# Attention block in f32: the softmax division pinned behind the fifth key block's running sum, and v's products laid in seven of the fourth head's eight key blocks

## The chip, the cores and the metric

The kernel runs on one core of a Trainium2 chip. The metric is the device time of one execution in microseconds (us); lower is better. Times are medians of several runs of one program, and the profile is of one further execution of it.

The engines' names are those of the profile: PE is the tensor engine (PEld its weight loads), DVE the vector engine, ACT the scalar engine, POOL the GpSimd engine, SP the sync engine. A "q" behind the name means the engine's sequencer, for instance one that issues a DMA.

## The reference

A group norm, an attention with four heads of 128 channels over 1024 positions, an output projection and a residual, for a batch of 16:

```python
# x: (16, 512, 32, 32) float32
xn = group_norm(x, 8 groups) * gamma + beta
q, k, v = split(einsum('oc,bchw->bohw', qkv_w, xn) + qkv_b)   # four heads of 128
attn = softmax(einsum('bhnd,bhmd->bhnm', q, k) * 128 ** -0.5, axis=-1)
out = einsum('bhnm,bhmd->bhnd', attn, v)
return x + einsum('oc,bchw->bohw', proj_w, out) + proj_b
```

The softmax's division can be done last: with p = exp(score), a head's output is (sum over m of p v) times 1 / (sum over m of p). That final multiplication is what this document calls the division.

## The kernel before

One loop runs over 16 batches x 4 heads x 8 key blocks of 128 keys. In each key block PE makes the scores of this block in two halves of 512 queries, ACT takes their exponentials, DVE adds them to a running sum `tot`, and PE multiplies the exponentials of the block before with v (`po`). Between these stand the products of the projections, cut into small units. They are made by Strassen's scheme in two levels: 4 groups of 7 units, each with sums of inputs on DVE, products into one of two kinds of PSUM bank (`x` and `y`), and evictions on ACT and DVE. Which units a head carries:

- first head (h = 0): q and k of this batch's second pair of heads
- second head (h = 1): the output projection of the batch before, and the norm of the next batch
- third head (h = 2): q and k of the next batch's first pair of heads
- fourth head (h = 3): v of the next batch

The parts that matter here, cut:

```python
    def scores(s, half):
        b, h, j = where(s)
        sc = ps_s.tile([P, HALF], F32, tag="s", name=f"s_{s}_{half}")
        nc.tensor.matmul(
            sc, ks[b, h][:, ts(j, P)], qs[b, h][:, ts(half, HALF)], start=True, stop=True
        )
        # ... (ps[s]: a tile for the exponentials of this block)
        nc.scalar.activation(ps[s][:, ts(half, HALF)], sc, AF.Exp, scale=SCALE)
        # ... (the sum follows the second half)
        if j == 1:
            tot[b, h] = lpool.tile([P, N], F32, tag="tot", name=f"tot_{b}_{h}")
            nc.vector.tensor_add(tot[b, h], ps[s - 1], ps[s])
        else:
            nc.vector.tensor_add(tot[b, h][:, i], tot[b, h][:, i], ps[s][:, i])

    def denominators(b, h):
        # DVE: two transposes, a reduction, small sums and a reciprocal of tot -> r, 32 x 32
        # ...
        inverse[b, h] = r

    def spread_inverse(b, h, step):
        if step == 0:      # to DRAM as one row
            row = rows_of[b, h] = dpool.tile([1, N], F32, tag="row", name=f"row_{b}_{h}")
            nc.scalar.dma_start(
                row.rearrange("o (c i) -> (o c) i", i=BLK), inverse.pop((b, h))
            )
            return
        rinv[b, h] = lpool.tile([P, N], F32, tag="rinv", name=f"rinv_{b}_{h}")
        nc.scalar.dma_start(rinv[b, h], rows_of.pop((b, h)).to_broadcast((P, N)))

    def divide(b, h):
        nc.vector.tensor_mul(os_[b, h], os_[b, h], rinv.pop((b, h)))

    def spread(plan, units, first, last):
        for i, u in enumerate(units):
            plan[first + i * (last - first) // len(units)].append(u)
```

One unit of a projection, and what follows a group of units:

```python
            def inner_sum(m):           # sums of inputs, tiles qk_t, pp_t; v loads kept ones
                # ...
                for i in range(n):
                    nc.vector.tensor_sub(have[m][:, i, :], inner(i, a), inner(i, c))

            def out_(which, a, c=None):  # eviction of a bank, tiles qk_r, pp_r, v_r
                # ...
                if c is None:
                    nc.scalar.copy(dst, view(a))
                else:
                    nc.vector.tensor_add(dst, view(a), view(c))

            return [
                unit(weights, lambda: inner_sum("t1"), lambda: inner_sum("t2"), p1),
                unit(lambda: inner_sum("t3"), p2), unit(lambda: inner_sum("t4"), p6),
                unit(lambda: load(g + 1, "t2"), p5), unit(lambda: load(g + 1, "t1"), p7),
                unit(lambda: load(g + 1, "t3"), p4),
                unit(lambda: load(g + 1, "t4"), p3, end),
            ]
```

`weights` loads the group's weights from DRAM into one of two buffers. When v's groups are combined, each finished block goes through a sum (`vt`), a transpose on DVE (`vu`), a write to DRAM and two loads back (`v_groups`, cut here).

What a head carries, and the main loop:

```python
    def plan_head(b, h):
        plan = [[] for _ in range(NB)]
        if h == 0:
            spread(plan, staggered(next_qk.pop()), 0, NB)
            if b > 0:
                plan[6].append(lambda: o_blocks(b - 1))
                plan[6].append(lambda: sums_of_b(ob[b - 1]))   # DVE sums of o, the tiles ot
        # ...
        elif h == 2:
            spread(plan, staggered(qk_groups(b + 1, 0)), 0, NB)
        else:
            spread(plan, staggered(next_v.pop()), 0, NB)
        return plan

    for s in range(steps + 1):
        # ... (units = plan[j] of this head)
        if 0 < s < steps and s % NB == 0:
            denominators(*where(s - 1)[:2])
        for half in range(NH2):
            if s < steps:
                scores(s, half)
                if j == 1 and s > NB:
                    spread_inverse(*where(s - NB)[:2], half)
                if half == 0 and j == 5 and s > NB:
                    divide(*where(s - NB)[:2])
            if s > 0:
                weighted_sum(s - 1, half)
            n = (len(units) + 1) // 2
            run(units[half * n : (half + 1) * n])
```

So the division of a head is written in key block j = 5 of the head that follows it. The order in which an engine gets its instructions is not the written one: it is set when the kernel is built, by the operands' dependencies and the build's own estimate of when each instruction can go. `tc.issue_after(instruction)` adds a demand to it: what is written inside comes later than that instruction on its engine.

Of the kernel before, what the change touches and what calls it, by code (L numbers as in the profile page):

```python
# [154 lines left out]
def fast_path(ctx, tc, x, sources, out, consts, flag, dims):  # L155
# [6 lines left out]
    nc = tc.nc  # L162
    B, C, N, NCC, NH2, NB, GC, SCALE = dims
# [79 lines left out]
    def stats_group(b):  # L243
        mu, sc = norm.group(mvs.pop(b))
        scaled[b] = sc, norm.shift(mu, sc)
# [22 lines left out]
    def sums_of_b(b, rows=(1, 2), chunks=range(KC)):  # L268

        def sub(o, i, j):  # L270
            for k in chunks:
                nc.vector.tensor_sub(b[o][k], b[i][k], b[j][k])

        if 1 in rows:
            sub("t1", "b12", "b11")
        if 2 in rows:
            sub("t2", "b22", "t1")
            sub("t3", "t2", "b11")
            sub("t4", "b21", "t2")
# [6 lines left out]
    def o_blocks(b):  # L286
        ob[b] = halves([os_[b, h] for h in range(HEADS)], "o")
# [34 lines left out]
    def stage_blocks(site):  # L322

        raw = raw_blocks(site)
        st = stage[site] = {}
        names = ("a11", "a12", "a21", "a22", "s1", "s2")
        if site in ("proj", "v"):
            for n in names[:4]:
                st[n] = ypool.tile([P, HALF], F32, tag="y", name=f"st_{n}")
            for i, n in enumerate(names[4:]):  # L330
                st[n] = tpool.tile([P, HALF], F32, tag=f"ot2{i}", name=f"st_{n}")
        else:
            for i in range(3):
                t = opool.tile([P, N], F32, tag="o", name=f"st_{site}_{i}")
                for h in range(2):
                    st[names[2 * i + h]] = t[:, ts(h, HALF)]
        for n in names[:4]:
            load_block(st[n].rearrange("p (s d) -> p s d", d=P), raw[n])
# [66 lines left out]
    def run(units):  # L405
        for u in units:
            u()
# [270 lines left out]
    def proj_groups(b):  # L678

        def finish(which, r, a, c):  # L680
            of, half = int(which[1]) - 1, int(which[2]) - 1
            o = 2 * of + r
            t = ypool.tile([P, HALF], F32, tag="y", name=f"y_{b}_{o}_{half}")
            dma = nc.gpsimd.dma_start(t, x[b, ts(o, P), ts(half, HALF)])

            tc.add_manual_dep(
                dma.ins, last_eviction[b].ins.name,
                mybir.DependencyInfo(
                    mybir.DependencyClass.Sync, mybir.DependencyReason.DATA
                ),  # L690
                reason="residual",
            )
            nc.vector.scalar_tensor_tensor(
                t, a, projb_sb[:, o : o + 1], t, ALU.add, ALU.add
            )
            nc.vector.tensor_add(t, t, c)  # L696
            nc.gpsimd.dma_start(out[b, ts(o, P), ts(half, HALF)], t)  # L697

        return two_levels(f"pp_{b}", "proj", b, lambda: ob[b], finish)


    ps, tot, po, rinv, last_eviction = {}, {}, {}, {}, {}
    inverse, rows_of = {}, {}
    steps = B * HEADS * NB

    def where(s):
        bh, j = divmod(s, NB)
        return (*divmod(bh, HEADS), j)
# [7 lines that stand above are left out]
        if half == 0:  # L716
            ps[s] = ppool.tile([P, N], F32, tag="p", name=f"p_{s}")
        nc.scalar.activation(ps[s][:, ts(half, HALF)], sc, AF.Exp, scale=SCALE)  # L718
        i = ts(half, HALF) if s == steps - 1 else ds(0, N)
        if j == 0 or (half == 0 and s < steps - 1):  # L720
            return
        if j == 1:
            tot[b, h] = lpool.tile([P, N], F32, tag="tot", name=f"tot_{b}_{h}")
            nc.vector.tensor_add(tot[b, h], ps[s - 1], ps[s])
        else:
            nc.vector.tensor_add(tot[b, h][:, i], tot[b, h][:, i], ps[s][:, i])  # L726

    def denominators(b, h):

# [85 lines left out]
# [7 lines that stand above are left out]
# [20 lines left out]
    def staggered(lists):  # L842


        starts = (0, 4, 8, 16)[: len(lists)] if len(lists) != 3 else (0, 4, 10)
        at = [(a + i, g, u) for g, (a, us) in enumerate(zip(starts, lists))
              for i, u in enumerate(us)]
        return [u for _, _, u in sorted(at, key=lambda t: t[:2])]
# [98 lines left out]
# [7 lines that stand above are left out]
                plan[6].append(lambda: sums_of_b(ob[b - 1]))  # L954
            else:
                plan[5].append(lambda: stage_blocks("v"))
        elif h == 1:
            if b > 0:
                spread(plan, staggered(proj_groups(b - 1)), 0, NB)
            if b + 1 == B:  # L960
                plan[0].append(lambda: last_loads("x"))
            else:
                plan[0].append(lambda: load_x(b + 1))
                spread(plan, [lambda c=c: stats_chunk(b + 1, c) for c in range(NCC)], 2, 4)
                plan[4].append(lambda: stats_group(b + 1))
                for r in range(2):
                    plan[5 + r] += [
                        lambda c=c, half=half: normalise(b + 1, c, half)
                        for c in range(KC * r, KC * r + KC) for half in range(NH2)
                    ]  # L970
                    plan[6 + r].append(lambda r=r: x_sums(b + 1, (r + 1,)))
            if b == 0:
                for g in range(len(OUTER)):
                    plan[g // 2].append(lambda g=g: kept_group("v", g))
                    plan[NB // 2 + g].append(lambda g=g: kept_group("proj", g))
                plan[2].append(lambda: stage_blocks("proj"))
                spread(plan, [lambda o=o: bias_of_v(o) for o in range(NCC)], 3, 5)
        elif b + 1 == B:
            if h == 2:
                plan[0].append(lambda: last_loads("w"))  # L980
                plan[2].append(last_bias)
            else:
                os_[b, h] = opool.tile([P, N], F32, tag="o", name=f"o_{b}_{h}")
                plan[3].append(lambda: o_blocks(b))
                plan[3].append(lambda: sums_of_b(ob[b], (1,)))
                plan[5].append(lambda: sums_of_b(ob[b], (2,), (0,)))
        elif h == 2:
            spread(plan, staggered(qk_groups(b + 1, 0)), 0, NB)
        else:
            spread(plan, staggered(next_v.pop()), 0, NB)  # L990
        return plan

    def warm(n, name):
# [26 lines left out]
    next_v, next_qk = [], [qk_groups(0, 1)]  # L1020
# [3 lines left out]
    plan = []  # L1024
    for s in range(steps + 1):
        units = []
        if s < steps:
            b, h, j = where(s)
            if j == 0:
                plan = plan_head(b, h)  # L1030
            units = plan[j]
            if j == NB - 1 and h > 1 and b + 1 < B:
                (next_v if h == 2 else next_qk).append(
                    v_groups(b + 1) if h == 2 else qk_groups(b + 1, 1)
                )
                if h == 2:
                    units.append(ahead[f"v_{b + 1}"])
# [4 lines that stand above are left out]
                scores(s, half)  # L1042
                if j == 1 and s > NB:
                    spread_inverse(*where(s - NB)[:2], half)
                if half == 0 and j == 5 and s > NB:
                    divide(*where(s - NB)[:2])
            if s > 0:
                weighted_sum(s - 1, half)
            n = (len(units) + 1) // 2
            run(units[half * n : (half + 1) * n])  # L1050
        if s > 0:
            del ps[s - 1]
# [134 lines left out]
```

## Time and profile before

| what | value |
|---|---|
| time, median of 3 runs | 3317.27 us (3309.16 to 3321.45) |
| span of the profiled execution | 3309.1 us |
| PE busy | 3198.2 us, 97% |
| DVE busy | 2659.2 us, 80% |
| ACT busy | 1446.6 us, 44% |
| POOL busy | 527.0 us, 16% |
| granted clock of PE | 0.998 |

A row of the costliest groups names the line, the engine, the operation, the tiles written and read and their shape, how often, the busy time in us with the mean of one in ns, and behind the second bar how long the engine sat idle just before these instructions and what ended most of that. A row of the waits names the engine and tile that waited, what it waited for, the total in us, how many times, and the longest. A row of a timeline has the start and the length in us, the instruction, and in brackets the idle time before it with what ended it. A row of the stretches has the window, its length, the busy time and number of instructions of PE, PEld, DVE, ACT and POOL, the clock, the share of the DMA engines and GB/s. A product's record is longer than the distance to the next product, [...] so busy PE is not the same as PE at its peak.

### The profile page before, as it was taken

The page shows a single profiled execution, that of the slowest core. Times are in us where ns is not written, and L with a number is a line of the kernel's source. Part 1 is how long each engine was busy: PE and PEld are TensorE (multiplying, and loading weights), DVE is VectorE, ACT ScalarE, POOL GpSimd, SP SyncE. Part 2 cuts the span into 40 slices and gives each one's busy share as a digit, 9 for nine tenths or more (in the row PEclk, how much of TensorE's full clock was granted, in tenths as well). Part 3 has the DMA queues.
Part 4 walks back from the last instruction along what each step waited for, and adds up shares of the span by engine and source line. Part 5 has one row for each costly group of instructions (what it writes and reads, how often), then busy time and mean ns, then how long its engine had stood idle before and what let it go on. Part 6 is the DMA issues. An engine that isn't in the chain of part 4 may idle for free. (4 is left out here: it accounts for less than half of the span.)

```text
span 3309.1 us, 33607 instructions
## 1 busy us (share of the span) xinstructions
PE 3198.2 (97%) x10474; PEld 2165.8 (65%) x10474; DVE 2659.2 (80%) x4609; ACT 1446.6 (44%) x2709; POOL 527.0 (16%) x938
## 2 busy tenths in 40 slices
PE   8999999999999999999999999999999999999999
PEld 6566666666666666666666666666666666666664
DVE  8878878788887888878888787887878878788784
ACT  2534435344353443534435354353534535344342
POOL 1011121111211112111121101212012121121100
PEclk9999999999999999999999999999999999999999
DMA  5555454545535455454554545545355463454631
GB/s 202 196 187 151 169 177 145 168 150 172 176 133 171 144 172 177 154 159 139 171 174 154 172 136 179 170 147 179 127 176 175 144 204 126 160 162 162 189 124 39
DMA packets 172664, 530.54 MB, mean 160 GB/s; under 512 B 28864, under 2 KB 51904, under 8 KB 172480
## 3 DMA queue, kind: packets, MB, share of 16 engines
q1 hardware_dynamic: 91120, 276.86, 25.5%
q0 software_dynamic: 67392, 216.07, 20.3%
q10 hardware_dynamic: 13968, 35.41, 3.5%
q8 instruction: 85, 1.39, 0.2%
q14 instruction: 99, 0.81, 0.1%
HBM read 389.56 MB, written 138.67 MB: 160 GB/s over the span
## 5 line engine op out<-in xcount | busy, mean ns | idle before, releaser
L806 PE MATMUL po<-p,v 128*128 128x512 f32 x2048 | 1053.8, 596 | 0.0
L713 PE MATMUL s<-qk,qk 128*128 128x512 f32 x2048 | 1049.1, 594 | 2.9 <-ACT p L718 2.9
L718 ACT ACTIVATE p<-s 128x512 f32<-128x512 f32 x1024 | 610.5, 597 | 992.6 <-PE s L713 982.5
L806 PEld LDWEIGHTS po<-p,v 128*128 128x128 f32 x2048 | 600.8, 303 | 315.3 <-issue 197.6
L726 DVE TENSOR_TENSOR tot<-tot,p 128x1024 f32<-128x1024 f32 x385 | 470.4, 1222 | 116.6 <-ACT p L718 114.5
L713 PEld LDWEIGHTS s<-qk,qk 128*128 128x128 f32 x2048 | 388.2, 190 | 91.4 <-issue 28.7
L510 PE MATMUL qk_x<-qk_t,w 128*128 128x256 f32 x1344 | 361.5, 386 | 3.4 <-ACT qk_u L421 2.1
L510 PEld LDWEIGHTS qk_x<-qk_t,w 128*128 128x128 f32 x1344 | 246.1, 190 | 175.9 <-issue 65.4
L421 ACT COPY qk_u<-qk_x 128x512 f32<-128x512 f32 (+1 forms) x256 | 136.3, 533 | 287.5 <-PE qk_x L510 245.5
L499 POOL DMA_DIRECT2D kept_t<-qk_t x256 | 138.8, 543 | 491.2 <-DVE qk_t L495 457.1
L660 POOL DMA_DIRECT2D vd<-vu x120 | 66.5, 554 | 827.0 <-DVE vu L652 766.7
L529 DVE TENSOR_TENSOR qk_r<-qk_y,qk_u 128x512 f32<-128x512 f32 (+1 forms) x256 | 158.7, 620 | 47.4 <-ACT qk_u L421 26.4
L510 PE MATMUL pp_x<-pp_t,w_proj 128*128 128x256 f32 x630 | 173.9, 389 | 3.0 <-ACT pp_u L421 3.0
L529 DVE TENSOR_TENSOR v_r<-v_y,v_u 128x512 f32<-128x512 f32 (+1 forms) x120 | 75.1, 626 | 124.0 <-ACT v_u L421 116.3
L510 PE MATMUL qk_y<-qk_t,w 128*128 128x256 f32 x448 | 128.9, 393 | 45.9 <-DVE qk_t L495 30.6
L697 POOL DMA_DIRECT2D out_y<-y x120 | 66.4, 554 | 653.5 <-DVE y L696 620.7
L510 PEld LDWEIGHTS v_x<-v_t,w_v 128*128 128x128 f32 x630 | 118.4, 190 | 79.1 <-issue 38.3
L510 PE MATMUL v_x<-v_t,w_v 128*128 128x256 f32 x630 | 166.6, 381 | 0.0
L510 PEld LDWEIGHTS pp_x<-pp_t,w_proj 128*128 128x128 f32 x630 | 113.8, 190 | 69.8 <-ACT pp_u L421 24.8
L665 POOL DMA_DIRECT2D v<-vd x240 | 140.3, 592 | 52.1 <-issue 47.3
L510 PEld LDWEIGHTS qk_y<-qk_t,w 128*128 128x128 f32 x448 | 80.8, 191 | 101.6 <-DVE qk_t L495 41.4
L816 DVE TENSOR_TENSOR o<-o,rinv 128x1024 f32<-128x1024 f32 x63 | 77.0, 1223 | 86.7 <-DMA rinv<-row 86.7
(204 smaller groups left out, 4537.6 us busy)
## 6 DMA issues: line engine op xcount, KB each, us to landing
w<-kept SPq DMA_DIRECT2D x90, 896.0 KB, 6.1
kept_t<-qk_t POOLq DMA_DIRECT2D x192, 256.0 KB, 2.8
v_t<-kept_t SPq DMA_DIRECT2D x180, 256.0 KB, 2.7
w_v<-kept_v SPq DMA_DIRECT2D x45, 896.0 KB, 4.9
w_proj<-kept_proj SPq DMA_DIRECT2D x45, 896.0 KB, 4.5
rinv<-row ACTq DMA_DIRECT2D x63, 512.0 KB, 4.5
x<-in_x POOLq DMA_DIRECT2D x60, 512.0 KB, 5.7
vd<-vu POOLq DMA_DIRECT2D x120, 256.0 KB, 2.6
```

Source lines behind the costliest of these rows:

```text
L421: nc.scalar.copy(t[n][:, :width], t["x"][:, :width])
L499: nc.gpsimd.dma_start(t, have[m][:, :n])
L510: nc.tensor.matmul(acc[:, ts(i, Q)], have["w"][:, i, SLOTS[an], :], inner(i, bn), start=(first and i == 0), stop=True, skip_group_check=True,)
L529: nc.vector.tensor_add(dst, view(a), view(c))
L660: nc.gpsimd.dma_start(rows[which][ts(h, P), :], u)
L665: nc.gpsimd.dma_start(vs[b, pair][ts(q, BLK), half].rearrange("m h (k i) j -> m (h k) (i j)", k=n), rows[which].rearrange("(k m) (q e) -> ...
L697: nc.gpsimd.dma_start(out[b, ts(o, P), ts(half, HALF)], t)
L713: nc.tensor.matmul(sc, ks[b, h][:, ts(j, P)], qs[b, h][:, ts(half, HALF)], start=True, stop=True)
L718: nc.scalar.activation(ps[s][:, ts(half, HALF)], sc, AF.Exp, scale=SCALE)
L726: nc.vector.tensor_add(tot[b, h][:, i], tot[b, h][:, i], ps[s][:, i])
L806: nc.tensor.matmul(po[b, h][:, i], v_block(b, h, j), ps[s][:, i], start=(j == 0), stop=(j == NB - 1),)
L816: nc.vector.tensor_mul(os_[b, h], os_[b, h], rinv.pop((b, h)))
```

## The change

Two things. The division is written in key block 4, behind the second half's scores, and pinned on DVE behind the running sum of that block, so that it can come no earlier in DVE's order. It is meant to keep DVE from standing still in front of a division whose inverse is still on its way. And the 28 units of v, which were spread over all eight key blocks of the fourth head, are spread over the first seven, so that v's last sums and transposes on DVE come earlier against the start of the next batch.

```diff
     ps, tot, po, rinv, last_eviction = {}, {}, {}, {}, {}
-    inverse, rows_of = {}, {}
+    inverse, rows_of, added = {}, {}, {}
 ...
-            nc.vector.tensor_add(tot[b, h][:, i], tot[b, h][:, i], ps[s][:, i])
+            added[b, h, j] = nc.vector.tensor_add(
+                tot[b, h][:, i], tot[b, h][:, i], ps[s][:, i]
+            )
 ...
         elif h == 2:
             spread(plan, staggered(qk_groups(b + 1, 0)), 0, NB)
         else:
-            spread(plan, staggered(next_v.pop()), 0, NB)
+
+            spread(plan, staggered(next_v.pop()), 0, NB - 1)
 ...
-                if half == 0 and j == 5 and s > NB:
-                    divide(*where(s - NB)[:2])
+                if half == 1 and j == 4 and s > NB:
+
+                    with tc.issue_after(added[b, h, 4].ins):
+                        divide(*where(s - NB)[:2])
```

## The prediction

> **What bounds the kernel now.** I read the page's busy times first, then what the tensor engine (PE) waited for, then the four heads of one batch as stretches of time, then the timelines of PE and the vector engine (DVE) inside them. The page:
>
> ```profile
> PE 3198.2 (97%) x10474; PEld 2165.8 (65%) x10474; DVE 2659.2 (80%) x4609; ACT 1446.6 (44%) x2709; POOL 527.0 (16%) x938
> ...
> L816 DVE TENSOR_TENSOR o<-o,rinv 128x1024 f32<-128x1024 f32 x63 | 77.0, 1223 | 86.7 <-DMA rinv<-row 86.7
> ```
>
> PE is the bound and nothing in the change alters its products, so all that can be won is PE's idle time. Line 816 is the division: DVE sat idle 86.7 us ahead of it, for the broadcast inverse to land. That is DVE's idle time, not yet PE's. The view of PE's own waits says which waits reach PE:
>
> ```profile
> PE qk_y L510 <- DVE qk_t L495: 30.6, 27, 3.0
> PE qk_x L510 <- DMA w<-kept: 21.6, 20, 2.0
> PE qk_y L510 <- DVE qk_r L529: 19.0, 15, 3.6
> ...
> PE v_y L510 <- DVE v_r L529: 5.5, 15, 0.4
> ```
>
> (total us, times, longest.) To see where they stand I cut batch 5 into its four heads; each row gives the stretch, its length and the engines' busy times.
>
> ```profile
> 1071.67:1124.90 53.23, 49.44 (x163) 33.76 (x162) 44.43 (x81) 19.04 (x34) 11.54 (x21) 1.00 0.58 167
> 1124.90:1175.20 50.30, 50.00 (x167) 34.37 (x166) 42.44 (x80) 34.07 (x70) 7.07 (x12) 1.00 0.36 125
> 1175.20:1226.40 51.20, 50.00 (x164) 33.47 (x164) 43.66 (x78) 19.16 (x34) 9.76 (x18) 1.00 0.54 184
> 1226.40:1275.70 49.30, 48.94 (x163) 34.21 (x162) 35.27 (x50) 19.15 (x34) 5.98 (x11) 1.00 0.54 169
> ```
>
> All four heads hold about 49 us of PE work. The fourth (v's products) is practically full; the first loses 3.8 us. From all records I took the distance between starts of consecutive products beyond its usual value (429 ns for 512 columns, 215 ns for 256) and sorted it by head: about 61 us in the first heads, 25 in the second, 58 in the third, 13 in the fourth. In the first heads of batches 1 to 15 it falls on three places:
>
> *Stall A*, 8.1 us into the head, about 1.63 us, in all fifteen. PE and then DVE in batch 5:
>
> ```profile
> 1077.26 1.02 PE L713 MATMUL s<-qk,qk 128*128 128x512 f32 x2
> 1079.74 0.70 PE L510 MATMUL qk_y<-qk_t,w 128*128 128x256 f32 x2 [1.46 <-DVE qk_t L495]
> ```
> ```profile
> 1076.19 1.13 DVE L652 STREAM_TRANSPOSE vu<-vt 128x512 f32<-128x512 f32 x1
> ...
> 1078.28 1.09 DVE L652 STREAM_TRANSPOSE vu<-vt 128x512 f32<-128x512 f32 x1
> ...
> 1079.27 0.41 DVE L495 TENSOR_TENSOR qk_t<-x 128x256 f32<-128x256 f32 x1
> ```
>
> From 1061.3 to 1087.1 DVE has hardly a gap; the inner sums stand behind the last transposes of v.
>
> *Stall B*, about 22 us in, 0.5 to 3.7 us, 17 us in all:
>
> ```profile
> 1087.06 0.42 DVE L495 TENSOR_TENSOR qk_t<-xt,qk_t 128x256 f32<-128x256 f32 x1
> 1092.38 1.23 DVE L816 TENSOR_TENSOR o<-o,rinv 128x1024 f32<-128x1024 f32 x1 [4.90 <-DMA rinv<-row]
> 1093.64 0.69 DVE L272 TENSOR_TENSOR ot<-o,o 128x512 f32<-128x512 f32 x1
> 1094.25 0.68 DVE L529 TENSOR_TENSOR qk_r<-qk_y,qk_p 128x512 f32<-128x512 f32 x1
> ```
> ```profile
> 1094.99 1.13 PE L510 MATMUL qk_y<-qk_t,w 128*128 128x256 f32 x4 [2.33 <-DVE qk_r L529]
> ```
>
> The code asks for the division in the sixth key block, yet here it runs after one running sum only; it holds the eviction qk_r, and PE needs the bank that this frees.
>
> *Stall C*, about 26 us in, the second-next weights (w<-kept): 6 us over 15 heads.
>
> By head, DVE's waits ahead of the division are 51 us in the first heads (1.6 to 6.1 each), 28 in the fourth (1.4 to 2.3, except 0.2 in the last batch), 7 elsewhere. Those in the fourth heads cost PE nothing: DVE has 14 us of idle time there, nearly all of it before 27 us. In batches 1 to 14 the second and third heads' divisions hardly ever wait.
>
> [...] ready evictions pass at 1094.25, only after the division. [...] here the row's write has a median of 3.5 us with the two directions mixed, and the broadcast 4.5 us. [...] the division's row has 1223. Neighbours overlap: what follows the division starts 1.13 to 1.26 us after it. So the division costs DVE about 1.14 us wherever it stands; only the wait can go.
>
> **The change, part by part.**
>
> *The pin.* No instruction is added. 63 divisions of 1.22 us stay. The division now follows the running sum of key block 4, at about 33 us of a head (1107.68 + 1.22 against 1071.67 is 37 in the delayed first head; 1055.18 + 1.27 against 1022.3 is 34 in batch 4's fourth). The inverse landed at about 20.7 us in the first (1092.38) and 12.8 us in the fourth (1035.09): the wait disappears, 80 of 86.7 us. PE's gain is stall B, 17 us. But C lies 4 us behind B and its load runs during it. In the third heads, without B, C is 1.0 to 2.2 us; the first heads have one more pair of products (0.86 us) between the weights' last use and their next, so I expect 0.4 to 0.6 us where it is 0.4 on average now: give back 3 us. Net 14 us.
>
> *The division's 1.14 us in its new place.* First heads: DVE has 3 us of gaps between 24 and 33 us and 0.9 between 36 and 45; with the wait gone the whole chain is earlier, so the division and three sums behind it (L272, 0.6 us each) fit. The proj sums that need them start in the next head. Third heads: 3 us of gaps after 33 us, free. Second heads: it leaves the loose part and enters the dense one (0.9 us idle between 33 and 50); maybe 0.2 us per batch. Fourth heads: DVE is dense from 28 us on (0.7 us of idle time to the head's end). Here 1.1 us are added to the very chain that ends in stall A, and up to 1.8 if the sums follow.
>
> *v in seven blocks.* 28 units, 3.5 per block before, 4 in blocks 0 to 6 after; PE's work is the same, but v ends one block without units earlier: 8 products of 429 ns, 3.4 us. DVE's v chain starts its dense stretch about an eighth of 21 us, 2.6 us, earlier. Without the pin this removes all of A (1.46) and of the v_y wait (0.37). With the pin: 2.6 − 1.14 + 0.5 of small gaps absorbed = 2.0 us against 1.83 needed; with the three sums close behind, 0.2. The sums are wanted only in the next head and can slip, so I take 1.2 us per batch, 15 × 1.2 = 18 us. From that I take 5 us for v_y waiting longer on a denser DVE in blocks 4 to 6, and 3 us for the second heads.
>
> Sum: 14 + 18 − 8 = 24 us. 3317.3 − 24 = 3293.
>
> **The rivals.** (1) *The pin only moves the delay*: the division in the fourth head cancels the seven blocks, A stays and v_y waits grow by 1 us a batch; 14 − 15 = no change, 3318. For it: DVE's gapless stretch after 28 us. Against: the sums need not follow at once. (2) *The weights take B's place*: C grows to the third heads' 1.4 us, giving back 15 us; then only A's part is left, 3305. For it: batch 11 has no B and a C of 2.05; against: batches 12 and 13 have no B and C of 0.42 and nothing. (3) *All goes*: A, B and v_y, and a freer DVE shortens the qk_t waits of the third heads too: 22 + 17 + 5 + 8, 3265. (4) The order of all engines is made anew when the kernel is built; other places can shift by 10 us either way.
>
> **Range and chances.** Rivals 1 and 3 bound it, with 10 us of reordering: 3270 to 3322. 2% is 66 us; the four waits of PE quoted above are 77 us together and half of them are untouched, so faster by over 2% gets 0.03; a slowdown of 66 us would need 4 us a batch of new stalls, also 0.03.
>
> **What would show it.** DVE's idle time ahead of line 816 near zero; the wait of qk_y for qk_r down from 19.0 to under 5 us; that for qk_t from 30.6 to about 13; that for w<-kept between 20 and 28; v_y for v_r between 3 and 12; first heads near 50 us (52.2 on average now), fourth heads 49.3 to 50. Wrong if fourth heads grow by over 1 us, or qk_t's wait stays at 30.

## The result, and the profile after

The changed kernel takes 3283.01 us (median of 4 runs, 3279.09 to 3288.52) against 3319.36 us for the kernel before beside it: a ratio of 0.9894, 95% interval 0.9863 to 0.9924. The prediction said 3293 with 3270 to 3322. The profiled executions have spans of 3281.3 and 3309.1 us.

What PE waited for after the change (total us, times, longest), then the division, which is on line 818 now, by its tile `rinv`. Under "its engine sat idle before it" there is no entry: DVE no longer waits in front of any division.

```profile
PE qk_x L510 <- DVE qk_t L495: 29.2, 16, 2.0
PE qk_x L510 <- DMA w<-kept: 22.4, 16, 2.4
...
PE v_y L510 <- DVE v_r L529: 9.0, 15, 0.6
...
PE qk_y L510 <- DVE qk_r L529: 0.5, 1, 0.5
```
```profile
L818 DVE TENSOR_TENSOR o<-o,rinv x63: 1192/1218/1224, 139.9 to 3235.8; 128x1024 f32<-128x1024 f32 x63
its engine sat idle before it (us, times) until:
who waited for it (us, times):
```

So the 86.7 us in front of the division are gone, and with them stall B: qk_y waited 19.0 us for qk_r and waits 0.5. But the wait for the inner sums qk_t, 30.6 us before, is still 29.2, now for the bank qk_x. Stall A has not gone.

The four heads of batch 5 as stretches of the changed kernel:

```profile
1061.44:1112.70 51.26, 49.21 (x163) 34.08 (x162) 42.91 (x76) 18.73 (x34) 11.29 (x21) 1.00 0.56 171
1112.70:1162.30 49.60, 49.22 (x165) 34.11 (x165) 41.87 (x83) 34.16 (x70) 7.06 (x12) 1.00 0.37 126
1162.30:1213.80 51.50, 49.93 (x165) 34.12 (x164) 44.48 (x80) 19.12 (x34) 9.76 (x18) 1.00 0.53 184
1213.80:1263.60 49.80, 49.20 (x165) 34.23 (x164) 35.05 (x50) 19.26 (x34) 6.28 (x11) 1.00 0.55 170
```

Over all batches, the distances between starts of consecutive products beyond their usual value, as in the prediction (429 and 215 ns; the records of these products are 592 and 379 ns long at the median), went like this (us in all):

| heads | before | after |
|---|---|---|
| first | 61.0 | 50.5 |
| second | 25.2 | 20.0 |
| third | 57.8 | 39.2 |
| fourth | 13.5 | 18.7 |
| sum | 157.5 | 128.4 |

The 29 us that they lost are the 28 us by which the spans differ. But most of it was not won where it was expected. The lengths of heads say less than these stalls, since two of PE's products (0.43 us by their usual distances) moved from each second head into the third head behind it. Stall A in batch 5 of the changed kernel, PE and then DVE (the head starts at 1061.44):

```profile
1066.60 1.03 PE L510 MATMUL qk_y<-qk_t,w 128*128 128x256 f32 x4
1069.57 1.48 PE L510 MATMUL qk_x<-qk_t,w 128*128 128x256 f32 x4 [1.94 <-DVE qk_t L495]
```
```profile
1046.86 1.21 DVE L818 TENSOR_TENSOR o<-o,rinv 128x1024 f32<-128x1024 f32 x1
...
1048.59 0.67 DVE L272 TENSOR_TENSOR ot<-o,o 128x512 f32<-128x512 f32 x1
1049.30 0.69 DVE L272 TENSOR_TENSOR ot<-ot,o 128x512 f32<-128x512 f32 x1
...
1050.51 0.68 DVE L272 TENSOR_TENSOR ot<-o,ot 128x512 f32<-128x512 f32 x1
...
1065.84 1.24 DVE L735 STREAM_TRANSPOSE tt<-tot 128x1024 f32<-128x1024 f32 x1
1067.00 1.08 DVE L652 STREAM_TRANSPOSE vu<-vt 128x512 f32<-128x512 f32 x1
1067.90 1.19 DVE L737 TENSOR_REDUCE part<-tt 128x32 f32<-128x1024 f32 x1
1068.98 0.44 DVE L495 TENSOR_TENSOR qk_t<-x,qk_t 128x256 f32<-128x256 f32 x1
```

The transpose `tt` and the reduction in the kernel before, where the head starts at 1071.67:

```profile
1073.36 1.24 DVE L733 STREAM_TRANSPOSE tt<-tot 128x1024 f32<-128x1024 f32 x1
...
1075.07 1.23 DVE L735 TENSOR_REDUCE part<-tt 128x32 f32<-128x1024 f32 x1
```

Two things are to be seen. The three sums of o (L272) do follow the division at once, in the fourth head. And the inner sum that PE waits for runs as late as before. In the kernel before, `tt` and the reduction ran 1.7 and 3.4 us into the head, v's last transpose ended at 7.7, and PE waited for the second inner sum, at 7.6. Now v's last transpose ends at 6.6, but the reduction has moved behind it, and PE waits for the third inner sum, at 7.5. Over the fifteen batches this wait grew from 22.0 to 28.0 us.

### The profile page after: what moved, and what is told of

It reads as the page before. It is cut to its first block, busy times and chain, and to the rows that moved or that the text cites. A ratio compares the mean times of both kernels' runs of the same rounds, so it can differ in the third digit from the quotient of the medians.

```text
span 3281.3 us, 33566 instructions
## 1 busy us (share of the span) xinstructions
PE 3188.9 (97%) x10474; PEld 2177.4 (66%) x10474; DVE 2636.7 (80%) x4609; ACT 1447.4 (44%) x2709; POOL 526.9 (16%) x938
## 4 chain that ended last, share of the span: by engine, by line
PE 74%; DVE 15%; DMA 6%; issue 2%; ACT 2%; POOL 0%; SPq 0%; DVEq 0%; POOLq 0%; ACTq 0%
PE po L808 20%; PE s L713 20%; PE qk_x L510 11%; PE qk_y L510 7%; DMA w<-kept 5%; PE pp_x L510 4%; PE v_x L510 4%; PE v_y L510 3%; PE pp_y L510 3%; DVE vu L652 3%; DVE tot L726 2%; DVE vt L649 2%; ACT x L82 1%; DVE v_r L565 1%; DVE v_r L529 1%
## 5 line engine op out<-in xcount | busy, mean ns | idle before, releaser
L510 PE MATMUL qk_x<-qk_t,w 128*128 128x256 f32 x1344 | 361.0, 385 | 31.6 <-DVE qk_t L495 29.2
L665 POOL DMA_DIRECT2D v<-vd x240 | 140.3, 592 | 53.1 <-issue 51.7
L510 PE MATMUL qk_y<-x,w 128*128 128x256 f32 x512 | 142.8, 381 | 0.0
L421 ACT COPY v_u<-v_x 128x512 f32<-128x512 f32 (+1 forms) x124 | 66.3, 535 | 165.0 <-PE v_x L510 125.6
L597 DVE SCALAR_TENSOR_TENSOR qk<-qk_r,qkb_sb,qk_r 128x512 f32<-128x512 f32 x192 | 137.0, 740 | 1.1
```

What stands on the lines that cost most here:

```text
L421: nc.scalar.copy(t[n][:, :width], t["x"][:, :width])
L510: nc.tensor.matmul(acc[:, ts(i, Q)], have["w"][:, i, SLOTS[an], :], inner(i, bn), start=(first and i == 0), stop=True, skip_group_check=True,)
L597: nc.vector.scalar_tensor_tensor(st[b, h][:, ts(half, HALF)], a, qkb_sb[:, i : i + 1], c, ALU.add, ALU.add)
L665: nc.gpsimd.dma_start(vs[b, pair][ts(q, BLK), half].rearrange("m h (k i) j -> m (h k) (i j)", k=n), rows[which].rearrange("(k m) (q e) -> ...
```

## The experiments

Two theories were put against each other for stall A. The **chain** theory is the prediction's: DVE's gapless work in the fourth head overruns the head's end, and A is as long as the overrun. The **order** theory: A is set by which instructions stand ahead of the inner sums in DVE's order, however much work came earlier. All kernels below compute the whole reference; ratios are to the kernel before in the same group of runs.

### Each part alone

pin_only takes the seven blocks back; v7_only takes the pin back:

```diff
-            spread(plan, staggered(next_v.pop()), 0, NB - 1)   # pin_only
+            spread(plan, staggered(next_v.pop()), 0, NB)
```
```diff
-                if half == 1 and j == 4 and s > NB:            # v7_only
-                    with tc.issue_after(added[b, h, 4].ins):
-                        divide(*where(s - NB)[:2])
+                if half == 0 and j == 5 and s > NB:
+                    divide(*where(s - NB)[:2])
```

> The pin alone, v in all eight blocks. Chain theory (stall A, at the start of each first head, is as long as the vector engine's gapless chain in the fourth head overruns; the division, 1.13 us, and the three sums of o that follow it, 0.6 us each, lengthen that chain by 2.9 us): stall B gone, but stall A grows from 1.46 to 3 to 4 us in each of 15 batches, and the v_y wait grows too; 3300 to 3325 us, ratio 0.995 to 1.002. Order theory (A is set by where the inner sums stand in the vector engine's order, behind v's last transposes and the denominators, whatever stands before): A stays at 1.5 to 2 us, the pin gives the whole gain and the seven blocks nothing; 3283 us, ratio 0.989.

> v in seven blocks alone, no division pinned. Chain theory: v ends 3.4 us earlier and nothing is added, so A falls from 1.46 to under 0.5 us and the v_y wait stays under 6 us; B (17 us) and the 87 us of idle time ahead of the division stay: 3290 to 3300 us, ratio 0.992 to 0.995. Order theory: A stays at 1.5 to 2 us, 3315 to 3320 us, ratio 1.00.

Measured: pin_only 3325.65 us, ratio 1.0017 (1.0006 to 1.0027); v7_only 3310.75 us, 0.9963 (0.9949 to 0.9977). PE's waits of pin_only:

```profile
PE qk_y L510 <- DVE qk_t L495: 53.0, 15, 3.9
PE qk_x L510 <- DMA w<-kept: 21.4, 15, 2.5
```

and of v7_only:

```profile
PE qk_x L510 <- DVE qk_t L495: 33.8, 31, 2.2
```

Neither part is worth much alone, and together they give 1.1%. With the pin alone A grew from 1.46 to 3.5 us at the median of the 15 batches. That is the size the chain theory said, but only in part its reason: DVE also waited 18.6 us in all (1.24 a batch) ahead of v's transposes for buffers that a DMA was still writing out, a wait that the kernel before does not have. And this stall cost PE more than its own length. In batch 5, first PE, then the stretch behind the stall (its granted clock is the third figure from the end):

```profile
1084.99 1.22 PE L510 MATMUL qk_y<-qk_t,w 128*128 128x256 f32 x2 [3.54 <-DVE qk_t L495]
1086.00 1.91 PE L510 MATMUL qk_x<-qk_t,w 128*128 128x256 f32 x4
...
1088.75 1.03 PE L510 MATMUL qk_x<-qk_t,w 128*128 128x256 f32 x4
```
```profile
1084.60:1088.00 3.40, 3.01 (x7) 2.48 (x8) 3.40 (x14) 0.05 (x1) 3.40 (x7) 0.51 0.61 194
```

Four products take 1.91 us in this stretch, at a granted clock of 0.51, and 1.03 us a little later. Such stretches of 3.4 or 6.8 us begin in A or just behind it in 13 of the 15 first heads of pin_only, in 4 of 15 in the change (A 1.9 us) and in none of the kernel before (A 1.5 us). By the distances between products they cost the first heads 29.9 us in pin_only and 6.0 us in the change, so they are 23.9 of the 42.5 us by which these heads' stalls differ (93.0 and 50.5). Which lengths of a stall bring such a stretch was not tested.

With seven blocks alone A did not shrink, against the chain theory: it grew to 32.6 us in all, in two waits per batch, with 15.0 us of half clock in these heads on top. The time lies in neither of the two ranges expected. B had gone there too, without a pin (qk_r's wait 2.0 us): the new order put the division of first heads later by itself, and DVE's idle time ahead of it fell from 51 to 9 us in those heads.

### The division out of the fourth head

```diff
+                pinned = h in (0, 1, 2)
+                if half == 0 and j == 5 and s > NB and not pinned:
+                    divide(*where(s - NB)[:2])
-                if half == 1 and j == 4 and s > NB:
+                if half == 1 and j == 4 and s > NB and pinned:
```

> The changed kernel, but the division that runs in fourth heads is not pinned; it goes back to its early place, where the vector engine has idle time. Chain theory: 28 us of idle time ahead of the division come back and cost nothing; A falls from 1.94 to under 0.5 us, the v_y wait from 9.0 to under 6 us in total: 25 us less than the change, 3255 to 3262 us, ratio 0.981 to 0.983. Order theory: A stays at 2 us, same time as the change, ratio 0.989.

Measured: 3276.72 us, 0.9884 (0.9853 to 0.9914), not distinguishable from the change. The division and its three sums were back in the loose part of the fourth head (30.6 us of idle time ahead of it, harmless), v_y's wait was gone, and fourth heads took 49.10 us instead of 49.72. But A stayed, at 32.0 us in all against 28.0, mostly as two waits per batch:

```profile
1066.12 0.69 DVE L649 TENSOR_TENSOR vt<-v_r,v_r 128x512 f32<-128x512 f32 x1 [1.02 <-DMA vd<-vu]
1066.72 1.22 DVE L726 TENSOR_TENSOR tot<-tot,p 128x1024 f32<-128x1024 f32 x1
1067.86 1.08 DVE L652 STREAM_TRANSPOSE vu<-vt 128x512 f32<-128x512 f32 x1
1068.80 1.20 DVE L735 STREAM_TRANSPOSE tt<-tot 128x1024 f32<-128x1024 f32 x1
1069.92 0.38 DVE L495 TENSOR_TENSOR qk_t<-x,qk_t 128x256 f32<-128x256 f32 x1
```
```profile
1070.45 0.70 PE L510 MATMUL qk_x<-qk_t,w 128*128 128x256 f32 x2 [2.19 <-DVE qk_t L495]
```

Here 2.9 us less work stand in the chain, DVE even has a gap, and PE still waits 2.19 us. The gap is a new wait: v's sum vt needs one of four y buffers, and those of the transposes before are free only when their write to DRAM has landed: DVE waited for that 17 times, 10.0 us in all. Behind it the inner sum stands in line after tot, vu and tt.

### The sums of o held back

```diff
-                plan[6].append(lambda: sums_of_b(ob[b - 1]))
+                def late_sums():
+                    with tc.issue_after(added[b, 0, 5].ins):
+                        sums_of_b(ob[b - 1])
+                plan[6].append(late_sums)
```

> The changed kernel, with the sums of o (twelve of 0.69 us per batch) held back behind the sixth running sum of the first head, where their units are written, so that none stands in the fourth head. Chain theory: 1.8 of the 2.9 us go, A falls from 1.94 to 0.3 to 0.8 us: 3262 to 3270 us, ratio 0.983 to 0.985, if the second head still finds its sums in time. Order theory: A stays, 3283 us or more.

Measured: 3338.34 us, 1.0072 (1.0052 to 1.0092). A stayed (qk_x waited 33.2 us for qk_t), another miss of the chain theory. The sums are eight a batch, not twelve: in batch 5, six now run late in the first head and two at the start of the second. The kernel became slower in the second heads (29.5 us of stalls against 20.0 in the change) and the third (69.1 against 39.2), with 34.9 us of waits for weights against 22.4. Which of the moved instructions causes this was not taken apart.

### The denominators behind the inner sums

```diff
-        if 0 < s < steps and s % NB == 0:
+        if 0 < s < steps and s % NB == 0 and h > 0:
             denominators(*where(s - 1)[:2])
...
-                if j == 1 and s > NB:
+                if j == (2 if h == 0 else 1) and s > NB:
                     spread_inverse(*where(s - NB)[:2], half)
...
             run(units[half * n : (half + 1) * n])
+            if half == 0 and 0 < s < steps and s % NB == 0 and h == 0:
+                with tc.issue_after(summed[0].ins):     # the last inner sum written so far
+                    denominators(*where(s - 1)[:2])
```

> The changed kernel (all divisions pinned, seven blocks), but in first heads the denominators (tt, its reduction and the small steps, 2.3 us and more on the vector engine) are written behind the first two units of q and k and pinned behind their inner sums; the row and its broadcast are issued one key block later there. Order theory: stall A is the inner sums standing behind tt and the reduction, so it falls from 1.94 us by 1.1 to 2.2 us in each of 15 batches: PE's wait of qk_x for qk_t from 29.2 to under 12 us, 3255 to 3270 us, ratio 0.981 to 0.985. Chain theory (the sum of all work before counts, not its order): A is as long as before or longer, since ACT then waits for the later reciprocal: ratio 0.989 or more.

Measured: 3262.78 us, 0.9843 (0.9815 to 0.987). The wait for qk_t falls from 29.2 us to

```profile
PE qk_x L513 <- DVE qk_t L496: 5.8, 16, 1.2
```

First heads take 50.55 us against 51.70 in the change; second and fourth are the same. The division and the sums of o are still in the fourth head. So the order theory is right for A in the changed kernel. Not all of A was won, though: in first heads PE now waited 15.1 us for weights, where it waited 0.9 us in the change.

### v's sums out of the y buffers

```diff
-            t = ypool.tile([P, HALF], F32, tag="y", name=f"vt_{b}_{pair}_{h}_{half}")
+            t = lpool.tile([P, HALF], F32, tag="tt", name=f"vt_{b}_{pair}_{h}_{half}")
```

The tile of tt is written and read by DVE alone where v's sums use it, so no DMA has to free it: DVE's waits for vd<-vu, 10.0 us in pin_h012_v7, are gone in vt_own. vt_own does this on pin_h012_v7, vt_own_late_denoms does both this and the late denominators, after_vt does it on the changed kernel as it is, before_vt on the kernel before.

> As pin_h012_v7, but v's sums vt go to the tile of the denominators' transposes (tt) instead of one of the four y buffers, which only a landed DMA frees; so the vector engine's wait of vt for vd<-vu (10.0 us in all) goes. If that wait is what kept stall A at 2.2 us when the division had left the fourth head, A falls by 0.7 to 1.0 us in 15 batches: ratio 0.984 to 0.986. If A is set by order alone (the inner sums behind tt, which cannot start before the last running sum), A stays over 1.7 us and the ratio is 0.987 to 0.989.

> Both: fourth-head division unpinned, vt out of the y buffers, denominators of first heads behind the inner sums. Order theory: A under 0.5 us, PE's wait of qk_x for qk_t under 8 us, ratio 0.979 to 0.982. Chain theory without order: like vt_own.

> The changed kernel as it is (all divisions pinned, seven blocks), but v's sums vt in the tile of tt instead of the y buffers. In the new order of the vector engine the third inner sum of a first head stands ahead of v's last transpose and of tt, as in vt_own; the division and the three sums of o stay in the fourth head's chain. Order theory: A is gone or under 0.5 us although the chain is 2.9 us longer: qk_x's wait for qk_t under 8 us, 3250 to 3262 us, ratio 0.981 to 0.985. Chain theory: A keeps 1 us or more, and v_y waits 9 us: ratio 0.986 to 0.989.

> The kernel before (no pin, eight blocks) with vt in the tile of tt. The trace of before has no wait for vd<-vu, so if the y buffers act through that wait alone, nothing changes: A 1.5 to 1.7 us, B 17 us, ratio 0.998 to 1.002. If they act through the order that the build makes, A falls below 1 us: ratio 0.992 to 0.996.

Measured: vt_own 3251.5 us, 0.9816 (0.9784 to 0.9849), the lowest of all and better than both kernels (its interval overlaps that of late_denoms); vt_own_late_denoms 3268.4 us, 0.986 (0.9825 to 0.9895); after_vt 3281.58 us, 0.9899 (0.9861 to 0.9937); before_vt 3348.28 us, 1.0101 (1.0067 to 1.0136).

None of the four times lies in a range that was expected. In all four stall A is gone: no wait for qk_t in first heads' beginnings is left. The buffer is not the only reason: with another tile the build made another order. In vt_own's DVE (its head starts at 1051.86) the inner sum stands ahead of v's last transpose and of tt:

```profile
1055.59 0.43 DVE L495 TENSOR_TENSOR qk_t<-x,qk_t 128x256 f32<-128x256 f32 x1
1055.91 1.11 DVE L652 STREAM_TRANSPOSE vu<-vt 128x512 f32<-128x512 f32 x1
1056.86 0.42 DVE L495 TENSOR_TENSOR qk_t<-x,qk_t 128x256 f32<-128x256 f32 x1
1057.18 1.23 DVE L735 STREAM_TRANSPOSE tt<-tot 128x1024 f32<-128x1024 f32 x1
```

That order does it shows in before_vt: the kernel before had no wait for a y buffer, and A went all the same. But there the unpinned division took the gain and more. Its inverse came later (in batch 5 the reciprocal starts 11.4 us into the head instead of 8.4), DVE idled 81.7 us ahead of it in first heads (51 before), half-clock stretches cost these heads 23.6 us, and B grew to

```profile
PE qk_y L510 <- DVE qk_r L529: 54.3, 17, 6.5
```

after_vt is the other lesson: A gone, and no time won. Its largest waits are

```profile
PE qk_x L510 <- DMA w<-kept: 38.6, 23, 3.1
PE v_y L510 <- DVE v_r L529: 12.2, 15, 0.8
```

where the change had 22.4 and 9.0. In first heads PE waited 16.5 us for weights (0.9 in the change) and another 7.9 us, 16 times, for ACT's evictions `qk_u`. Per batch, first heads won 0.76 us and third and fourth gave back 0.37 and 0.43. vt_own, which differs from after_vt by its text in the fourth head's division alone, takes 200.0 us per batch against 202.4, with first heads of 49.50 and fourth of 49.32 against 50.94 and 50.15. So here taking the division out of the fourth head's dense part does pay: v_y's wait is 4.7 us against 12.2, and in first heads the waits for weights fall from 16.5 to 4.9 us. That the shorter chain does this, and not again another order, is not shown. In vt_own_late_denoms, with A already gone, the later denominators gained nothing, and PE's wait for weights was 34.6 us against 26.2.

### Which heads need the pin, and the seven blocks

pin_h0_v7 pins first heads alone (`pinned = h in (0,)`), pin_h012_v8 is pin_h012_v7 with v in all eight blocks.

> Seven blocks, the division pinned in first heads alone. If the shorter second heads of the changed kernel (50.3 to 49.6 us each) come from the division leaving its place between the projection's evictions, they are back at 50.3 us here: against pin_h012_v7 10 us slower from them, and up to 10 us more from third heads: 3286 to 3297 us, ratio 0.991 to 0.994. If they come from something else of the new order, the time is that of pin_h012_v7, ratio 0.988.

> Pinned in all but fourth heads, v in all eight blocks, vt in the y buffers as before. If the seven blocks are needed only because the pin puts the division into the fourth head (pin_only: A 3.5 us), then here A is 1.5 us as in before, B is gone and second and third heads are as short as in the change: 3280 to 3288 us, ratio 0.988 to 0.991, as good as pin_h012_v7. If the seven blocks help by themselves, pin_h012_v7 is at least 8 us better: ratio 0.991 to 0.996.

Measured: pin_h0_v7 3300.38 us, 0.9957 (0.994 to 0.9974); pin_h012_v8 3292.42 us, 0.9923 (0.99 to 0.9946). Second heads took 50.42 us before, 50.37 in v7_only, 49.95 in pin_h0_v7, 49.60 with all pins. The last step is no gain of theirs: it is the two products that moved into the third heads. Beyond the usual distances of its products a second head lost 1.89 us before, 1.85 in v7_only, 1.43 in pin_h0_v7 and 1.50 in pin_h012_v7, so what they won came with the first heads' pin. A third head lost 3.69 us before, 3.63 in pin_h0_v7 and 2.80 in pin_h012_v7: that came with the pins of the second and third heads. The time of pin_h0_v7 lies in neither of its two ranges.

In pin_h012_v8 A is that of before, 1.63 us by the distance of the products (in batch 5 v's last transpose ends 7.71 us into the head in both), and B is gone, but the weights' wait is

```profile
PE qk_x L510 <- DMA w<-kept: 33.5, 25, 2.9
PE qk_y L510 <- DVE qk_t L495: 22.0, 15, 1.5
```

against 20.7 in pin_h012_v7. In first heads it is 15.0 us, against 5.2 in the kernel before: here the weights did take B's place. So A and B are as the first expectation has them, but the time lies in the range of the second. The intervals of the two (0.99 to 0.9946, 0.9853 to 0.9914) overlap, so whether seven blocks help when the division is out of the fourth head stays open. With it in the fourth head they are needed: 1.0017 without, 0.9894 with them.

### The weights in halves

The wait that is left in vt_own is the one for weights.

```diff
-            nc.sync.dma_start(w[:, : len(group)], store[site, g])
+            for i in range(len(group)):
+                nc.sync.dma_start(w[:, i], store[site, g][:, i])
```

> As vt_own, with each group's weights loaded as one transfer per product of the group (448 KB) instead of one of 896 KB, on the same queue, so that the first product can start when its own half has landed. If what is left in first and third heads is the first half's landing (rows of before: 448 KB in 3.3 us, 896 KB in 6.1), PE's wait for w<-kept falls from 26.2 to under 12 us: 3232 to 3245 us, ratio 0.976 to 0.980. If both halves share the queue and land together, the wait stays over 22 us and the ratio is that of vt_own, 0.980 to 0.984.

Measured: 3266.54 us, 0.9842 (0.9823 to 0.986), no faster than vt_own; the two intervals overlap. The halves' landing and the wait (issues with their size and the median time to landing, then PE's wait):

```profile
w<-kept SPq DMA_DIRECT2D x210, 448.0 KB, 4.2
```
```profile
PE qk_x L511 <- DMA w<-kept: 42.8, 32, 3.3
```

The 4.2 us are the median of all. Of two halves the first landed 3.9 us after its issue, where a single 448 KB took 3.3, and the second 5.5 us after the first one's issue, where the whole took 5.1 in vt_own. The wait grew from 26.2 to 42.8 us. The order of other engines changed with it, so this says that the edit doesn't help, not how much of that the transfers are to blame for.

## Why the prediction was right

The time lies in the range, 10 us below the 3293 us that were forecast. In the total this was in part luck, since two errors cancelled: the 18 us expected of A did not come, and 24 us came in second and third heads where a loss of 3 had been expected. One of the prediction's own signs of being wrong came true, since the wait for qk_t stayed at 29.2 us, and first heads took 51.7 us, not about 50.

- **The wait ahead of the division, stall B.** Expected to go, 17 us. Right: DVE's 86.7 us are 0, and qk_r's wait fell from 19.0 to 0.5. v7_only adds that B was tied to one order: another order that put the division later removed it without a pin. (The write of the row alone, which the prediction gives as 3.5 us mixed with the broadcast, has a median of 1.8 us in the kernel before.)
- **The weights give back 3 us (C).** Wrong in sign for first heads: PE's wait there fell from 5.2 to 0.9 us. In third heads it rose from 16.4 to 21.4. As a rival ("the weights take B's place") it did not happen in the change, but it did in pin_h012_v8, and in after_vt and late_denoms the weights took about half of what A had been.
- **v in seven blocks removes 1.2 us of A per batch, 18 us.** This step failed. A went from 1.46 to 1.94 us in batch 5. The sum behind it, 2.6 − 1.14 + 0.5, treated DVE's fourth head as a chain whose work only had to start earlier, and took it that the inner sums follow v's last transpose. That did end 1.1 us earlier, but the build put the reduction between it and the inner sum, so this ran as late as before. pin_h012_v7 took 2.9 us out of the chain and left A at 2.2; late_denoms left the chain and moved the order, and the wait for qk_t fell from 29.2 to 5.8 us.
- **The three sums of o can slip.** Wrong: they followed the division within 2 us, in the fourth head, although their results are wanted in the next. By the prediction's own sum the seven blocks then save 0.2 us and not 1.2, so this alone undoes most of the 18 us. In pin_late_sums the sums did slip, and A did not shrink.
- **v_y waits longer, up to 5 us.** Right: 5.5 to 9.0.
- **Second heads lose 3 us, third heads nothing.** Wrong: their stalls fell by 5.2 and 18.6 us. The wait of qk_y for qk_t some 9 us into the third heads (the twelve of the 27 waits that were not A) cost 10.5 us by the distances and went with the pins of second and third heads; pin_h0_v7 still has it (7.9 us, 14 times). Half-clock stretches in third heads cost 3.5 us less. The second heads' gain came with the first heads' pin, so it is not the move of their own division, which the prediction reckoned with; why stays open.

Expected 24 us: 14 of B and C, 18 of A, less 8. Measured 28 to 36: about 17 of B and 5 of C, minus 6 of A, minus 6 of the half-clock stretches behind it, minus 5 in fourth heads, and 24 in second and third heads, nearly all of which the prediction had not seen (by the distances between products; these add up to the table's 29).

## What to carry to other kernels

When an instruction waits for a transfer, as the division did, look first at what stands behind it on its engine and who needs that. The idle time in front of it is not the cost: 51 us of it in first heads cost PE 17 us, and 28 us in fourth heads cost PE nothing. When a build orders instructions itself, an edit moves more than what it names: read the new order before reckoning with lengths, and pin the few instructions that a bound engine waits for ahead of those that nobody needs yet. Look for the wait that stands next in line before counting a stall as won: A was taken out of the changed kernel in two ways, and one of them (late_denoms) brought 0.5% while the other (after_vt) brought nothing. And look at the granted clock behind long stalls, since a stall there can cost more than its length: in pin_only the half-clock stretches cost the first heads 29.9 us on top of A's 53.0 us of waits.

## What the runs showed of the hardware that was not expected

In the busy stream of PE's products, waits of a few microseconds were followed by stretches of 3.4 or 6.8 us in which PE was granted half the clock (0.51 in the one shown of pin_only, 0.50 from 1476.0 to 1478.4 us in the change). They came with A in 13 of 15 first heads where PE waited 3.5 us (pin_only), in 4 of 15 at 1.9 us (the change), and in none at 1.5 us (the kernel before). The length of the wait is not all: with 2.2 us a batch, mostly in two waits, it was 9 of 15 in v7_only and 3 of 15 in pin_h012_v7.

Of two transfers of 448 KB issued on one queue 0.37 us apart, the first landed after 3.9 us at the median and the second 5.5 us after the first one's issue, against 3.3 us for one alone and 5.1 us for a single one of 896 KB in vt_own.

A buffer of 256 KB that went out to DRAM was not free until the write had landed (2.6 us at the median in the kernel before). With four such buffers DVE waited 10.0 us for them in pin_h012_v7 and 18.6 us in pin_only, and not at all in the kernel before and the change.
